# First SAGE pass of a graph network: stored turned blocks in place of transposes, seven masks in the first slots, one adjacency test moved to the gated part

## The chip, the cores and the metric

The kernel runs on one core of a Trainium2 chip. The metric is the device time of one execution in microseconds. The median of three runs of the kernel before is 2209.74 us (2208.95 to 2210.49).

## The reference

Input are 16 graphs of 1024 nodes with 128 features each, `x`, and their adjacency matrices `adj` (0 or 1, float32, not symmetric). Two layers follow each other. The first is a gated graph network: four rounds in which messages are summed over the adjacency and go through a GRU cell, then a residual sum and a layer norm. The second first thins the adjacency row by row ("neighbour skipping") and then runs three SAGE layers with batch norms over all graphs, a linear head, and again a residual sum and a layer norm.

```python
def _dilate_pattern(adj_bool, mask_b):
    def step(carry, n):
        row = carry[n]; num = sum(row)
        sf = where(num > 10, (num + 1) // 2, 1)
        rm = row & (cumsum(row) % sf == 0)          # only where num > 1
        carry[n] = row & ~rm
        carry[:, n] = carry[:, n] & ~rm             # later rows lose these too
    ...
def _sage(x, adj, Wr, Wx, b, mf):
    deg = clip(sum(adj, -1), 1.0)
    out = (adj @ x / deg) @ Wr + x @ Wx + b
    return out / max(norm(out), 1e-12) * mf
h = x
for i in range(4):
    h = gru_cell(adj.T @ (h @ weight[i]), h, ...)
x = layernorm(x + h * mask)
adj_d = adj * keep(adj)                             # the skipping
h1 = bn(relu(_sage(x, adj_d, ...))); h2 = ...; h3 = ...
out = layernorm(x + (concat(h1, h2, h3) @ Wl + bl) * mf)
```

An entry of the thinned matrix survives only if both its own row and the row of its column keep it. That is why both a block and its mirror image, turned, are needed.

## The kernel before

The work falls into five stages. Inside each the order of the instructions on every engine is the order in which the code emits them, so the tables and `if t in (...)` lines below are the schedule.

*Gated part* (0 to 1281 us). Two streams of graphs take turns; `Gated.layer` emits one layer of one stream. A layer is some 19 us, 64 layers in all. At ten places of a layer (`aside(n)`) one step of the skipping, `FixPoint.steps`, is emitted. The skipping works on blocks of 128 rows of four graphs at once (32 blocks of 20 steps, so a block lasts two layers): `keep` applies the removals that earlier rows of the graph have caused, from the tile `f_rt` (tile `left[i, g]`, 128 rows by k x 128 columns for block k); `count` scans; later `rows` writes the result `f_nr` to DRAM (`e_nr`, L867): +0.5 for an entry that its row keeps, -0.5 for one that it removes, 0 where there was no edge. `read_last` (L723) and `read_back` (L716) fill the next block's `f_rt` with DMA transposes of what earlier blocks wrote. There are four `f_rt` buffers. The kernel computes the skipping with a fixed point and with the assumption that `adj` holds only 0 and 1. `look` (L1982, VectorE, 128x1024) tests that assumption on a tile of 128 rows of `adj`; two of the eight tiles of a graph are tested in the gated part (`load_test`, `check`; tile `h_test`, one per layer of the second stream), six in the first SAGE pass (`load_a`, `check`; tile `p_a`).

*First SAGE pass* (`Sage.first`, 1281 to 1748 us). It runs over graphs, 16 slots for each: `slot(b, t)` emits slot t of graph `b` ("now") and at the same time prepares graph `n = b + 1` ("next"). The slots of b = -1 only prepare graph 0; this is the prologue. To prepare a graph is: load `e_nr` (`load_nr`, tile `p_nr`) and the rows (`load_s`, tile `p_s`); in `unit`, TensorE turns 128x128 blocks (four into one PSUM bank `p_u`, 16 units a graph, L1482); ScalarE writes the part above the diagonal into the thinned, transposed matrix `p_at` (L1487); in `unit_low` VectorE masks the rest (L1495: one input from `p_nr`, one from the PSUM bank); GpSimd packs each half row block to bytes (`pack`, L1503, tile `p_b`) for the later passes; the rows are normed, turned and split into a high and a low part (`p_xh`, `p_xl`). For "now", TensorE multiplies `p_at` with `p_xh` and `p_xl` (`agg`, L1564), then `out_first`, and then a chain goes through VectorE `scale_rows` (L1388, L1389), ScalarE `squares`, VectorE `rows` (L1402 to L1407), `split_r` on ScalarE and GpSimd (`p_rh`, `p_rl`), back to TensorE for the second aggregation (`agg` with `p_rh`, `p_rl`), and `turn_r`. `constants` and `first_weights` prepare weights; `load_given` loads them.

*Second and third pass and the head* (1748 to 2206 us) are not touched.

SyncE (SP) issues nearly all DMAs of the SAGE passes, in the order of the code; an issue that waits for a buffer holds up those behind it.

## Time and profile before

| what | value |
|---|---|
| median of three runs | 2209.74 us |
| the profiled execution's own time | 2207.94 us |
| its span, first to last instruction | 2206.2 us |
| granted TensorE clock, mean | 0.986 |
| busy: PE, DVE, ACT, POOL | 2099.8, 1836.0, 1327.2, 1233.9 us |
| gated part | 0 to 1281 us |
| first SAGE pass (prologue to 1296) | 1281 to 1748 us |
| second, third pass, head | 1748 to 2000, 2130, 2206 us |

PE is TensorE, PEld its weight loads, DVE VectorE, ACT ScalarE, POOL GpSimd, SP SyncE. A line such as `L1495 DVE ... p_at<-p_nr,p_u 128x512 fp32r<-128x512 bf16 x72 | 48.2, 673 | 3.5` is a group of 72 instructions of line 1495 that write `p_at` from `p_nr` and `p_u`; together they are busy 48.2 us, one takes 673 ns on average, and before them the engine was idle 3.5 us in all. Consecutive instructions of an engine may overlap by some 0.05 to 0.09 us.

### The profile page before, as it was taken

How to read it: one execution, taken by the hardware profiler on the slowest of the kernel's cores; microseconds unless marked ns; L12 is line 12 of the kernel's file. 1: busy time of each engine (PE TensorE's matmuls, PEld its weight loads, DVE VectorE, ACT ScalarE, POOL GpSimd, SP SyncE). 2: the span in 40 equal slices, each digit the busy share in tenths (PEclk: the TensorE clock that was granted, in tenths of full speed). 3: DMA queues.
4: the chain of work that ended last, by engine and by line, in shares of the span. 5: the costliest groups of instructions: out<-in, count | busy, mean ns of one | idle time of the engine just before them, and what ended most of it. 6: DMA issues, size and time to landing. Idle time of an engine off the chain costs nothing. (4 is left out here: it accounts for less than half of the span.)

```text
span 2206.2 us, 32924 instructions
## 1 busy us (share of the span) xinstructions
PE 2099.8 (95%) x10217; PEld 1441.5 (65%) x10217; DVE 1836.0 (83%) x4213; ACT 1327.2 (60%) x3238; POOL 1233.9 (56%) x1218
## 2 busy tenths in 40 slices
PE   6999999999999999999999979999999899999987
PEld 4666556666666665666655657777777678887865
DVE  4898998889998889989889978888888666766877
ACT  3657466565656666465575656666666355555756
POOL 4458558567476475585575457777777255540002
PEclk9999999999999999999999989999999999999989
DMA  8247446366364394472584178888887577764404
GB/s 254 76 107 244 90 115 223 85 179 184 84 202 129 80 256 110 91 241 78 126 237 101 52 263 309 304 306 306 305 305 259 210 249 248 248 225 171 139 30 143
DMA packets 233853, 406.13 MB, mean 184 GB/s; under 512 B 79042, under 2 KB 100196, under 8 KB 233668
## 3 DMA queue, kind: packets, MB, share of 16 engines
q1 hardware_dynamic: 187844, 284.37, 39.4%
q0 software_dynamic: 41472, 117.46, 19.8%
q10 hardware_dynamic: 4352, 2.11, 0.4%
q8 instruction: 83, 1.36, 0.2%
q14 instruction: 102, 0.84, 0.1%
HBM read 313.48 MB, written 109.25 MB: 192 GB/s over the span
## 5 line engine op out<-in xcount | busy, mean ns | idle before, releaser
L1104 PE MATMUL h_g<-h_h,h_wh 128*128 128x512 f32 x768 | 396.1, 597 | 3.3 <-DVE h_r L1116 3.3
L1104 PE MATMUL h_g<-h_ms,h_wi 128*128 128x512 f32 x768 | 392.2, 592 | 0.0
L1123 POOL TENSOR_TENSOR h_zh<-h_r,h_h 128x512 f32<-128x512 f32 x126 | 174.2, 1382 | 257.2 <-ACT h_r L1119 254.0
L737 DVE TENSOR_TENSOR_SCAN f_rank<-f_a,f_first,f_pd 128x1024 f16<-128x1024 bf16 x128 | 299.4, 2345 | 4.2
L1092 PE MATMUL h_g<-h_a,h_hi 128*128 128x512 f32 x1024 | 278.7, 413 | 1.0 <-DMA h_a<-in_adj_dram 0.9
L1503 POOL CAST p_b<-p_at 128x512 uint8<-128x512 f32 x256 | 219.8, 881 | 84.7 <-DVE p_at L1495 52.7
L1104 PEld LDWEIGHTS h_g<-h_ms,h_wi 128*128 128x128 f32 x768 | 145.5, 190 | 184.3 <-issue 168.9
L1092 PE MATMUL h_g<-h_a,h_lo 128*128 128x512 f32 x1024 | 261.8, 392 | 0.0
L1092 PEld LDWEIGHTS h_g<-h_a,h_hi 128*128 128x128 f32 x1024 | 190.1, 188 | 61.7 <-issue 22.2
L1396 ACT ACTIVATE s_junk<-s_o 128x128 bf16<-128x128 f32 x384 | 114.0, 298 | 175.2 <-DVE s_o L1389 164.6
L1092 PEld LDWEIGHTS h_g<-h_a,h_lo 128*128 128x128 f32 x1024 | 189.8, 188 | 38.6 <-DVE h_lo L1030 0.4
L1104 PEld LDWEIGHTS h_g<-h_h,h_wh 128*128 128x128 f32 x768 | 133.3, 190 | 100.3 <-issue 72.7
L1125 POOL TENSOR_TENSOR h_h<-h_h,h_zh 128x512 f32<-128x512 f32 x126 | 179.9, 1428 | 9.9
L1119 ACT ACTIVATE h_r<-h_r,h_bi 128x512 f32<-128x512 f32 x128 | 92.4, 722 | 149.2 <-DVE h_r L1118 149.2
L1124 POOL TENSOR_TENSOR h_zh<-h_z,h_zh 128x512 f32<-128x512 f32 x126 | 162.1, 1287 | 9.9
L1095 ACT COPY h_ms<-h_g 128x512 f32<-128x512 f32 x128 | 73.8, 577 | 150.8 <-PE h_g L1092 150.6
L910 ACT ACTIVATE f_u<-f_rank,f_q 128x128 f16<-128x128 f16 (+7 forms) x128 | 110.6, 867 | 70.2 <-DVE f_rank L850 70.2
L1771 PE MATMUL q_ob<-s_wxp,q_xt 128*128 128x256 f32 x512 | 125.7, 390 | 0.3
L1982 DVE SCALAR_TENSOR_TENSOR p_junk<-p_a 128x1024 bf16<-128x1024 f32 x96 | 125.7, 1309 | 0.0
L1495 DVE SCALAR_TENSOR_TENSOR p_at<-p_nr,p_u 128x128 fp32r<-128x128 bf16 (+1 forms) x192 | 102.5, 543 | 19.4 <-ACT p_at L1487 12.6
L887 ACT ACTIVATE f_pd<-f_rank,f_q 128x128 f32<-128x128 f16 x128 | 59.1, 462 | 96.5 <-DVE f_q L701 93.4
L1413 POOL TENSOR_TENSOR q_rl<-s_r,q_rh 128x512 fp32r<-128x512 f32 x32 | 41.2, 1288 | 128.8 <-ACT q_rh L1412 105.8
(256 smaller groups left out, 4770.7 us busy)
## 6 DMA issues: line engine op xcount, KB each, us to landing
h_a<-in_adj_dram POOLq DMA_DIRECT2D x128, 512.0 KB, 9.2
p_a<-in_adj_dram SPq DMA_DIRECT2D x96, 512.0 KB
f_a<-in_adj_dram POOLq DMA_DIRECT2D x128, 256.0 KB, 6.5
e_nr<-f_nr SPq DMA_DIRECT2D x128, 256.0 KB
p_nr<-e_nr SPq DMA_DIRECT2D x32, 1024.0 KB
h_test<-in_adj_dram SPq DMA_DIRECT2D x32, 512.0 KB
s_at<-p_b SPq DMA_DIRECT2D x32, 512.0 KB
s_ag<-s_ag SPq DMA_DIRECT2D x64, 256.0 KB
```

Of the source, the lines that this page charges most:

```text
L737: nc.vector.tensor_tensor_scan(out, a, other[:, 0, 0:1].to_broadcast([P, N]), start, op0=ALU.add, op1=ALU.bypass)
L910: nc.scalar.activation(u[:, :n1], rank[:, g, :n1], AF.Abs, bias=q[:, 1, g:g + 1], scale=q[:, 0, g:g + 1])
L1092: nc.tensor.matmul(pm[f], part[:, j, :], st.adj[j][:, half[f]], start=(j == 0 and n == 0), stop=(j == NB - 1 and n == 1))
L1104: nc.tensor.matmul(pg, lhs, rhs, start=(i == 0), stop=(i == len(mm) - 1))
L1123: aid.tensor_tensor(d, r, h, ALU.subtract)
L1124: aid.tensor_tensor(d, z, d, ALU.mult)
L1125: aid.tensor_tensor(h, h, d, ALU.add)
L1396: self.nc.scalar.activation(junk, o[:, i, :], AF.Square, accum_out=ss[:, i:i + 1])
L1495: self.nc.vector.scalar_tensor_tensor(g["at"][:, j, c0:c0 + low], v[:, j, c0:c0 + low], 0.0, pu[:, :low], op0=ALU.is_lt, op1=ALU.is_lt)
L1503: self.nc.gpsimd.tensor_copy(g["b", f][:, j, :], g["at"][:, j, f * HF:(f + 1) * HF].bitcast(F32))
L1771: nc.tensor.matmul(pb[:, i], g["xt"][:, f, blk], self.wxp, start=(i % 2 == 0), stop=False)
L1982: nc.vector.scalar_tensor_tensor(junk, a, 0.0, a, op0=ALU.is_gt, op1=ALU.not_equal, accum_out=bad[:, c:c + 1])
```

## The change

The skipping stores, for each block, the `f_rt` tile that it used in a new DRAM tensor `e_vt`: after step 10 of a block `send` issues four DMAs from SP. The tile's buffer is so held until the DMA has read it.

The first pass loads, for a graph, the lower blocks and the diagonal ones from `e_nr` in eight DMAs of 128 rows, and the 28 turned blocks from `e_vt` in one. TensorE then turns only the 36 blocks on and below the diagonal, in 12 units. VectorE masks the eight diagonal blocks from PSUM as before (`unit_own`) and the rest of each row block, 128 to 896 columns, in one instruction from the two loaded tiles (`unit_low`, seven of them, both inputs in SBUF). `p_at` is eight tiles in place of one.

The slots are laid out anew by four tables: units 0 to 3 stand in slots 0 and 2, the seven masks in slots 0 to 4 and (the last) 10. `out_first`, `scale_rows`, `rows`, `split_r` and the second aggregation each come one or two slots earlier. Five tests a graph stay in the pass; the sixth goes to the gated part, where each layer of the second stream now tests two tiles while the graphs 0, 1, 4, 5, 8, 9, 12, 13 run, and one as before in the others. `load_given` stands at the start of the pass, `constants` in slot 8 and `first_weights` in slot 9 of the prologue (it was in slot 3 of graph 0); the copy of `mask48` moves from `first_weights` to slot 4 of graph 0. The stores of `s_ag`, `s_at`, `s_rt`, `s_x` stand in other slots.

```diff
+def below(k):
+    return k * (k - 1) // 2
...
+    def send(self, i):
+        k, b0 = self.todo[i]
+        if k:
+            for g in range(self.G):
+                self.nc.sync.dma_start(self.turned[b0 + g, :, below(k) * P:below(k + 1) * P],
+                                       self.left[i, g][:, :k * P])
...
-            rt = self.left.pop((i, g))
+            rt = self.left[i, g]
...
             self.count(i, 1, a[1], rank, pt)
+            self.send(i)
...
     def load_test(self, n):
-        if n < B * 2:
-            self.test = self.wk.tile([P, N], F32, name="h_test", bufs=1)
-            self.nc.sync.dma_start(self.test, self.adj[n // 2, n % 2 * P:(n % 2 + 1) * P, :])
+        for i in range(1 + (n % NB < NB // 2)):
+            b, k = self.todo.pop(0)
+            t = self.wk.tile([P, N], F32, name="h_test")
+            self.nc.sync.dma_start(t, self.adj[b, k * P:(k + 1) * P, :])
+            self.tests.append((t, b, k))
...
-            if n == 1 and s == 1 and not checked:
-                self.check(b0 // 2 * L0 + l)
-                checked.append(l)
+            if s == 1 and self.tests and n not in checked and (n == 1 or n == 0 and len(self.tests) > 1):
+                self.check()
+                checked.append(n)
...
     def load_nr(self, b, f):
...
+            for k in range(4 * f, 4 * f + 4):
+                self.nc.sync.dma_start(g["v"][k], self.not_r[b, k * P:(k + 1) * P, :(k + 1) * P])
+                if k == 4:
+                    self.nc.sync.dma_start(g["low"], self.turn[b])
...
+        first, end = max(4 * f, j), 4 * f + 4
         pu = self.ps2.tile([P, HF], F32, name="p_u")
-        for i in range(4):
+        for i, k in enumerate(range(first, end)):
...
+    def unit_own(self, b, j):
+        g, own = self.g[b], slice(j * P, (j + 1) * P)
+        self.mask(g["at"][j][:, own], g["v"][j][:, own], g.pop(("pu", j)))
+
+    def unit_low(self, b, j):
+        g = self.g[b]
+        self.mask(g["at"][j][:, :j * P], g["v"][j][:, :j * P], g["vt"][j])
...
+    UNITS = {0: (0, 1), 2: (2, 3), 5: (8,), 6: (9,), 7: (10,), 8: (11,), 9: (12,), 10: (13,), 11: (14,), 12: (15,)}
+    LOWER = {0: (1, 2), 1: (3,), 2: (4,), 3: (5,), 4: (6,), 10: (7,)}
+    PACKS = {1: (0, 1), 3: (2, 3), 4: (4,), 5: (5,), 6: (6, 8), 7: (9,), 8: (10,), 9: (11,),
+             10: (12,), 11: (7, 13), 12: (14,), 13: (15,)}
+    TESTS = {1: 3, 5: 4, 7: 5, 11: 6, 13: 7}
...
-            if t in (5, 7):
-                self.out_first(b, t // 7)
+            if t in (4, 6):
+                self.out_first(b, t // 6)
...
-            if t in (9, 10, 12, 14):
-                part = g["rl"] if t in (10, 14) else g["rh"]
+            if t in (8, 9, 11, 12):
+                part = g["rl"] if t in (9, 12) else g["rh"]
...
+        if (b, t) == (-1, 8):
+            self.constants()
+        if (b, t) == (-1, 9):
+            self.first_weights()
         if (b, t) == (-1, 11):
-            self.load_given()
+            self.load_mask()
...
-        if (b, t) == (0, 3):
-            self.first_weights()
+        if (b, t) == (0, 4):
+            nc.vector.tensor_copy(self.mask48, self.m48)
```

## The prediction, made before the changed kernel ran

> **What bounds the kernel now.** I read the page's parts 1 and 2, then the windows by stage, the waits of the first SAGE pass, and one period of that pass as a timeline of VectorE and of GpSimd.

> Windows view; columns are stretch, length, busy us of PE, PEld, DVE, ACT, POOL, granted clock, DMA share, GB/s:

> ```profile
> 15.00:20.00 5.00, 1.12 (x4) 0.72 (x4) 0.42 (x2) 0.00 (x0) 0.53 (x1) 1.00 1.13 385
> ...
> 90.50:109.60 19.10, 19.10 (x75) 11.61 (x73) 15.32 (x36) 13.48 (x24) 8.40 (x8) 1.00 0.20 66
> 109.60:128.30 18.70, 18.70 (x70) 11.57 (x69) 17.86 (x38) 8.91 (x17) 9.53 (x11) 1.00 0.52 95
> ...
> 594.20:613.30 19.10, 19.10 (x75) 11.61 (x73) 17.23 (x37) 14.62 (x26) 10.07 (x9) 1.00 0.28 91
> ...
> 1552.40:1580.10 27.70, 26.25 (x193) 20.96 (x192) 24.33 (x62) 17.84 (x51) 20.16 (x21) 1.00 0.88 299
> ```

> The gated part (0 to 1281 us) is TensorE's: its layers last 18.7 to 20.5 us and PE fills them, with DVE busy 15 to 19 us of each. The start is DMA's: between 5 and 25 us the DMA engines are full and PE waits for weights. The last row is one graph of the first pass (1296 to 1748 us; from one graph's scale_rows to the next's the intervals average 27.79 us). There PE (26.25), DVE (24.33) and DMA (0.88) are all nearly full, so none alone sets the period. PE's own rest, in the waits view of that pass over 16 graphs (us in total, times, longest), is the chain of scale_rows, squares, rows and split; the third line is graph 0's alone:

> ```profile
> PE p_ag L1564 <- POOL p_rl L1413: 12.2, 15, 0.9
> PE p_ag L1564 <- ACT p_rh L1412: 10.1, 16, 1.8
> ...
> DVE s_mask L1310 <- DMA p_a<-in_adj_dram: 2.8, 1, 2.8
> ```

> **The change part by part.**

> *Transposes.* A unit of four blocks takes PE 0.20 to 0.23 us from its start to the next operation's (1555.33 to 1555.53), 0.053 a block. 28 fewer: 1.5 us, so PE needs 24.8 us a graph. This is a gain only if nothing else holds the period.

> *DVE work.* One test of six leaves: 1.31 + 0.08 us. Groups by form, over 12.25 graphs:

> ```profile
> L1982 DVE SCALAR_TENSOR_TENSOR p_junk<-p_a 128x1024 bf16<-128x1024 f32 x75 | 98.3, 1310 | 0.0
> ...
> L1495 DVE SCALAR_TENSOR_TENSOR p_at<-p_nr,p_u 128x512 fp32r<-128x512 bf16 x72 | 48.2, 673 | 3.5 <-PE p_u L1482 3.5
> L1495 DVE SCALAR_TENSOR_TENSOR p_at<-p_nr,p_u 128x384 fp32r<-128x384 bf16 x25 | 13.6, 545 | 6.2 <-ACT p_at L1487 6.2
> L1495 DVE SCALAR_TENSOR_TENSOR p_at<-p_nr,p_u 128x256 fp32r<-128x256 bf16 x25 | 10.5, 421 | 1.5
> L1495 DVE SCALAR_TENSOR_TENSOR p_at<-p_nr,p_u 128x128 fp32r<-128x128 bf16 x25 | 6.8, 272 | 0.0
> ```

> The twelve masks of a graph now take 6.5 us. The same 36 blocks come as eight own blocks (8 x 0.27 = 2.2) and seven masks of 128 to 896 columns. On the line of the rows above (0.27, then 0.133 per 128 columns) the seven are 4.7 us; by the gated part's f_a masks, which like them read both inputs from SBUF, 5.2 (0.35 at 128 columns, 1.10 at 896). So masks rise by 0.4 to 0.9 and DVE's work goes from 24.33 to between 23.3 and 23.8; I take 23.6.

> *The new conflict.* The old masks read one input from SBUF and one from PSUM; the seven new ones read two from SBUF. Timeline of DVE (start, length, line, operation):

> ```profile
> 609.64 1.08 DVE L729 SCALAR_TENSOR_TENSOR f_a<-f_rt,f_a 128x896 bf16<-128x896 bf16 x1
> ...
> 1552.72 1.55 DVE L1982 SCALAR_TENSOR_TENSOR p_junk<-p_a 128x1024 bf16<-128x1024 f32 x1
> ...
> 1560.13 1.21 DVE L1982 SCALAR_TENSOR_TENSOR p_junk<-p_a 128x1024 bf16<-128x1024 f32 x1
> ```

> and of GpSimd at the same times:

> ```profile
> 609.97 1.89 POOL L1123 TENSOR_TENSOR h_zh<-h_r,h_h 128x512 f32<-128x512 f32 x1 [1.58 <-ACT h_r L1119]
> 611.94 1.27 POOL L1124 TENSOR_TENSOR h_zh<-h_z,h_zh 128x512 f32<-128x512 f32 x1
> ...
> 1559.95 1.87 POOL L1503 CAST p_b<-p_at 128x512 uint8<-128x512 f32 x1 [2.67 <-DVE p_at L1495]
> 1562.01 0.62 POOL L1503 CAST p_b<-p_at 128x512 uint8<-128x512 f32 x1 [0.19 <-DVE s_rdeg L1559]
> ```

> A pack that meets a test lasts 1.87 us where the next, beside masks that read PSUM, lasts 0.62; a test that meets a pack lasts 1.55 in place of 1.21; the f_a mask holds up h_zh by 0.6 us. So a DVE instruction with two SBUF inputs and a GpSimd one take turns. Each new mask can cost DVE nothing or one whole pack (0.6 us): 0 to 4.2 us a graph. I take half, 2.1, because packs of the columns just masked become ready exactly when the next mask starts. DVE's work is then about 25.7 us.

> *DVE's idle time.* Of 3.4 us a period, the timeline shows 0.90 for a mask waiting for ACT's half of p_at, which goes; 0.37 for p_rs, 0.21 for s_ss, 0.76 and 0.22 for s_rt and small gaps stay. With about 1.7 kept the period is 25.7 + 1.7 = 27.4 us. GpSimd is the cross-check: 16 packs of 0.6 and four splits of 1.28 are 14.7 us, and DVE's two-SBUF instructions (five tests 6.0, seven masks 4.7, two rows 1.4, small ones 0.8) 12.9; taking turns that is 27.6, less about 1 to 2 us because consecutive starts overlap by 0.05 to 0.09. So 26 is a floor and 27.4 plausible; PE, at 24.8, becomes a waiter.

> [...]

> *DMA.* Turned blocks and the lower parts of e_nr are 28 + 36 blocks, the 2 MB loaded before; one test less is 0.5 MB of about 8.3. At 27.4 us that is about 284 GB/s against 299. The rows of 256 and 512 bytes are few. SP issues some six more DMAs a graph at 0.3 to 0.45 us and is mostly idle. load_a waits on SP for a test's buffer, and behind it stand the stores of s_rt, s_ag and s_at; each buffer's test lies one slot or more earlier, so I charge nothing; if that cover went, pack 0 of the next graph would wait for its p_b buffer, some 2 us, with GpSimd 7.5 us idle in a period.

> *First weights.* Now they, with mask48's copy, sit inside graph 0: from its first p_xh matmul (1296.42) to its scale_rows (1314.66) it takes 18.2 us, a later graph 11.4. That excess of 6.8 goes, the 2.8 us wait of s_mask with it. But constants (2.7 us of DVE) and first_weights (2.9, with PE between) move into the prologue, ahead of the last masks; its DVE has 4.5 us of waits to hide them in, and the p_u banks hang on those masks. I add 2.5 us (0 to 4). Net -4.3.

> *Gated part.* 16 tests of 1.2 to 1.5 us come into layers of the second stream of graphs 0-1, 4-5, 8-9, 12-13. Such layers have 3.8 us of DVE idle (90.5 to 109.6: 19.10 less 15.32) beside 1.9 in the heavy ones (594.2), and stay PE-bound; the first such layer of each pair of graphs has 2.3 to 3.3. I charge 0.8 us in all; 0 to 8; 21 if the cover were gone. 112 sends (SP, 0.4 us each) stand behind the transposes into f_rt that they wait for, and read_back waits for their landing; but read_back waits for DVE's f_a anyway, tens of us later for most. Nothing, up to 3 us. At the start a second test tile, 0.5 MB, is loaded while DMA is full: 0.52 MB at 250 to 385 GB/s is 1.4 to 2.1 us before PE's first layer: +1.6.

> *Sum.* 15 x (27.4 - 27.79) = -5.9; -4.3; +0.8; +1.6: -7.8 us. The profiled execution took 2207.94 (span 2206.20); the median is 1.8 above. From the median: 2202 us.

> **The rivals.**

> *The port decides (slower).* If the masks wait for three quarters of a pack each (3.2 us; all of it, 4.2, is the bound), the period is 23.6 + 3.2 + 1.7 = 28.5 (29.5): 15 x 0.7 = +10.6, with -4.3 and +2.4: +8.7, 2218 us. Slower by over 0.2% it is from a period of 28.2 on. For it: GpSimd is busy 20.16 of 27.70, and its order puts p_xl, for which PE waits, behind packs. Against: a mask that directly follows another need not wait, since the pack of 1559.95 waited through two DVE instructions.

> *No conflict.* The masks cost what the p_at rows say: DVE 23.6 + 1.7 = 25.3, and PE, 24.8 with its present 1.4 us of waits, sets 26.2. 15 x -1.6 = -23.9, less 1.9: 2184 us. Against: the f_a row.

> *The period stays.* The loop of scale_rows, squares, rows and splits sets it as before: -4.3 + 2.4, 2208 us, no change that shows.

> *The gated part pays.* The tests push DVE past its idle time in half of the 16 layers, 10 us: 2212.

> **How the numbers follow.** Forecast 0.36, no conflict 0.17, period stays 0.13, port 0.27, gated 0.07. 0.2% is 4.4 us, about what a measurement can tell from no change. Faster: 0.17 and 0.33 of the forecast's 0.36, 0.50. Same: the rest of it and most of "stays", 0.15. Slower: 0.35. The range from 2181 to 2221 leaves out the tails of the first and the port case.

> **What would show it.** L1482 at 576 transposes, PE at about 25 us a period; the seven masks at 5 us or more in a graph, packs of p_b at over 1 us mean; scale_rows of graph 0 near 1311; 48 tests in the gated part, ending within 3 us of 1281. Wrong it would be if the period is under 26.5 or over 28.2, or if PE shows new waits in the gated part.

## The result: 2.65% slower, and where the 56 us are

The changed kernel takes 2265.65 us (median of four runs, 2263.84 to 2266.44) against 2209.34 for the kernel before: ratio 1.0265, 95% interval 1.0249 to 1.0281. The forecast was 2202, the range 2181 to 2221. The profiled execution of after took 2263.84 us (span 2261.6), 55.9 us more than that of before.

By stage, from the two traces. The gated stretch ends with the last layer's last sums (the expectations below call that the last layer's start); graph times run from one first p_xh matmul to the next:

| stage | before | after | difference | forecast |
|---|---|---|---|---|
| start to first gated aggregation | 33.7 | 35.1 | +1.4 | +1.6 |
| gated part from there | 1227.3 | 1239.2 | +11.9 | +0.8 |
| to its last turn | 18.8 | 19.1 | +0.3 | 0 |
| prologue of the first pass | 16.6 | 34.2 | +17.6 | +2.5 |
| graph 0 | 34.5 | 28.3 | -6.2 | -6.8 |
| graphs 1 to 14 | 389.4 | 413.4 | +24.0 | -5.5 |
| graph 15 and all behind it | 485.8 | 492.3 | +6.5 | -0.4 |

Of the last row, 5.8 us lie in graph 15 itself (to the first matmul of the next layer's weights: 29.7 before, 35.5 after).

Windows of after, columns as in the prediction (length, busy us of PE, PEld, DVE, ACT, POOL, granted clock, DMA share, GB/s):

```profile
15.00:20.00 5.00, 1.46 (x7) 0.77 (x5) 0.56 (x1) 0.00 (x0) 1.01 (x2) 1.00 1.13 380
91.90:111.00 19.10, 19.10 (x75) 11.61 (x73) 17.45 (x38) 13.44 (x23) 9.31 (x8) 1.00 0.23 76
600.10:619.20 19.10, 19.10 (x75) 11.59 (x73) 17.20 (x37) 14.59 (x26) 10.03 (x9) 1.00 0.31 108
1355.89:1384.40 28.51, 25.02 (x168) 19.50 (x166) 24.52 (x63) 17.26 (x52) 23.20 (x21) 1.00 0.81 277
1384.40:1414.45 30.05, 26.56 (x168) 20.58 (x166) 24.49 (x63) 17.27 (x52) 22.36 (x21) 0.94 0.77 263
```

The light layer of graph 1 (second row) still lasts 19.10, with the second test inside it: DVE 17.45 instead of 15.32. So the cover named in the prediction held there. The last two rows are two neighbouring graphs of the first pass. PE has its forecast 25 us, DVE 24.5. But the graph lasts 28.5 us where the clock is 1.00 and 30.05 where it is 0.94; nine of the graphs 1 to 14 are of the second kind. Before, PE's waits were 1.4 us a graph (1.41 on the mean of graphs 1 to 14); now they are 3.5, and over all sixteen the longest are:

```profile
PE p_ag L1600 <- POOL p_xl L1433: 31.2, 15, 2.8
PE p_u L1509 <- DVE p_at L1519: 12.5, 16, 0.9
PE p_ag L1600 <- ACT p_rh L1432: 11.8, 16, 1.4
```

The first line was not there before: PE stands 2.03 us in each of the graphs 1 to 14, waiting for p_xl. Groups by form of the pass (graphs 1 to 14):

```profile
L1536 POOL CAST p_b<-p_at 128x512 uint8<-128x512 f32 x224 | 243.0, 1117 | 34.2 <-issue 12.8 <-DVE p_sh L1558 7.2 <-DMA s_at<-p_b 5.2
L1519 DVE SCALAR_TENSOR_TENSOR p_at<-p_nr,p_u 128x128 fp32r<-128x128 bf16 x112 | 28.5, 274 | 15.0 <-ACT p_at L1513 15.0
L1519 DVE SCALAR_TENSOR_TENSOR p_at<-p_nr 128x640 fp32r<-128x640 bf16 x14 | 17.2, 1225 | 0.0
L1519 DVE SCALAR_TENSOR_TENSOR p_at<-p_nr 128x896 fp32r<-128x896 bf16 x14 | 15.0, 1072 | 0.0
```

Packs take 1117 ns on the mean, before 901; the seven masks sum to 5.76 us a graph, and the one of 640 columns takes longer than that of 896, so what stands beside it counts.

### The profile page after: what moved, and what is told of

It reads as the page before. It is cut to its first block, busy times and chain, and to the rows that moved or that the text cites. A ratio compares the mean times of both kernels' runs of the same rounds, so it can differ in the third digit from the quotient of the medians.

```text
span 2261.6 us, 32358 instructions
## 1 busy us (share of the span) xinstructions
PE 2094.8 (93%) x9769; PEld 1424.3 (63%) x9769; DVE 1879.0 (83%) x4261; ACT 1314.6 (58%) x3238; POOL 1287.3 (57%) x1218
## 3 DMA queue, kind: packets, MB, share of 16 engines
q8 instruction: 80, 1.31, 0.2%
## 5 line engine op out<-in xcount | busy, mean ns | idle before, releaser
L1536 POOL CAST p_b<-p_at 128x512 uint8<-128x512 f32 x256 | 273.2, 1099 | 56.1 <-DVE p_at L1519 20.8
L1142 POOL TENSOR_TENSOR h_zh<-h_z,h_zh 128x512 f32<-128x512 f32 x126 | 176.8, 1403 | 9.9
L1055 PEld LDWEIGHTS h_g<-ident,h_h 128*128 128x128 f32 x512 | 62.7, 142 | 74.8 <-issue 68.5
L2027 DVE SCALAR_TENSOR_TENSOR p_junk<-p_a 128x1024 bf16<-128x1024 f32 x80 | 108.7, 1359 | 0.0
```

The lines of the kernel that those rows point to most:

```text
L1142: aid.tensor_tensor(d, z, d, ALU.mult)
L1536: self.nc.gpsimd.tensor_copy(g["b", f][:, j, :], g["at"][j][:, f * HF:(f + 1) * HF].bitcast(F32))
L2027: nc.vector.scalar_tensor_tensor(junk, a, 0.0, a, op0=ALU.is_gt, op1=ALU.not_equal, accum_out=bad[:, c:c + 1])
```

## Experiments

Theories after the result: the loss is four separate things (a pool's edge in the prologue, the second tests in the gated part, a longer loop in the first pass, a lowered clock on top). Rivals: the sends pay the gated part, the weights' loads the prologue, and the conflict of masks and packs the pass. Ratios are to the kernel before, run on the same chip. In the code below `...` marks lines left out, and comments name the run that a line belongs to.

**own_pool**: a pool of their own for two tiles.

```diff
         self.wk = pool("h_wk", bufs=2)
+        self.tp = pool("h_tp", bufs=2)      # h_test and h_junk from here
...
```

> The changed kernel with h_test and h_junk in a pool of their own behind the gated part's work pool; same addresses, same instructions. Theory A (the second h_test moves the end of the gated part's work pool 4 KB up, from 160320 to 164416 bytes a partition, over the start of the first p_nr at 162912, and the first load of p_nr then waits for the last use of any tile of that pool, the store of h_x): load_nr starts within 5 us of the last e_nr store, as before (there 1267.59 after a store at 1263.41 to 1267.1), the time from the gated part's last turn to the first p_xh aggregation falls from 34.9 to 17-20 us, the whole to 2247-2252. Rival B (the weights' loads and first_weights, now inside the prologue, hold it): that stretch stays above 28 us and the whole above 2258.

Ratio 1.0185 (1.0163 to 1.0208), 2248.1 us. SP's timeline (start, us, issue) of before, after and own_pool, in this order; with after stands GpSimd's issue of the last store of h_x:

```profile
1263.41 3.71 SPq L867 DMA_DIRECT2D e_nr<-f_nr  x4
1267.59 0.96 SPq L1466 DMA_DIRECT2D p_nr<-e_nr  x2
```

```profile
1276.59 3.71 SPq L881 DMA_DIRECT2D e_nr<-f_nr  x4
1296.07 0.54 POOL L1090 DMA_DIRECT2D e_sum<-h_x  x1 [8.46 <-DVE h_x L1088]
1299.16 0.82 SPq L1491 DMA_DIRECT2D p_nr<-e_nr  x2
```

```profile
1278.52 3.72 SPq L881 DMA_DIRECT2D e_nr<-f_nr  x4
1282.74 2.26 SPq L1492 DMA_DIRECT2D p_nr<-e_nr  x5
```

In after the load stands 18.9 us behind the last store of e_nr: SP waits until the store of h_x, issued 3.1 us earlier, has landed (its waits on the stores of h_x: 18.5 us). In own_pool it stands half a microsecond behind. The prologue is 22.1 us instead of 34.2. What PE waited for in after:

```profile
1300.96 0.27 PE L1509 MATMUL p_u<-ident_b,p_nr 128*128 128x128 bf16 x1 [7.16 <-DMA p_nr<-e_nr]
1313.11 0.58 PE L1509 MATMUL p_u<-ident_b,p_nr 128*128 128x128 bf16 x4 [8.68 <-DVE p_at L1519]
```

Theory A is shown for 12.1 of the 17.6 us: the second h_test, 4 KB, pushed the work pool's end over p_nr's first bytes (by the addresses that the expectation gives), and the load into that ground waited for the last user of the whole pool. In mended, below, with one h_test and no pool of its own, the prologue is 22.0 us too. (The 22.1 miss the 17 to 20 foretold by 2; see before_early.)

**one_test** and **no_sends**: the two additions to the gated part, taken away one at a time.

```diff
-        for i in range(1 + (n % NB < NB // 2)):
-            b, k = self.todo.pop(0)
+        for b, k in [(n // 2, n % 2)]:          # one_test
...
-            self.send(i)                        # no_sends
```

> The changed kernel without the sixteen second tests of the gated part (k = 2 of each graph is left untested; two h_test buffers stay, so addresses are the same). Theory A (DVE's time for the second test is what the gated part pays): first aggregation to last layer's start falls from 1238.9 us to 1227-1230 (before: 1227.1), the whole to 2253-2257. Rival B (the 112 sends pay it, by the places they take on SP ahead of the read-backs and by their DMA): that stretch stays within 2.5 us of 1238.9, the whole above 2261.

> The changed kernel without the sends of turned blocks (the first pass reads as many bytes from e_nr in their place, in pieces of 1 KB, so its masks hold other values). Theory A (second tests on DVE pay): the gated stretch of 1238.9 us falls by at most 3, the whole to no less than 2261. Rival B (sends pay): it falls by 8 to 12, to 1227-1231, the whole to 2253-2258.

In no_sends the first pass reads as many bytes from e_nr as it read from e_vt, so its masks hold other values. one_test: ratio 1.0202 (1.0182 to 1.0222), gated stretch 1228.7. no_sends: 1.0244 (1.0223 to 1.0265), stretch 1241.6. The second tests pay, all of it as far as the runs can tell; the sends cost nothing that shows. (Over all runs the stretch is 1238.8 to 1244.3 with the second tests and 1227.0 to 1229.4 without, with sends or not.) DVE at the end of graphs 8 and 9, before and then after:

```profile
792.05 1.30 DVE L1982 SCALAR_TENSOR_TENSOR h_junk<-h_test 128x1024 bf16<-128x1024 f32 x1
803.36 1.14 DVE L729 SCALAR_TENSOR_TENSOR f_a<-f_rt,f_a 128x512 bf16<-128x512 bf16 x1 [1.91 <-DMA f_rt<-f_nr]
```

```profile
797.22 2.00 DVE L2027 SCALAR_TENSOR_TENSOR h_junk<-h_test 128x1024 bf16<-128x1024 f32 x1
801.08 1.74 DVE L2027 SCALAR_TENSOR_TENSOR h_junk<-h_test 128x1024 bf16<-128x1024 f32 x1
812.97 1.75 DVE L742 SCALAR_TENSOR_TENSOR f_a<-f_rt,f_a 128x512 bf16<-128x512 bf16 x1 [2.50 <-DMA f_rt<-f_nr]
```

Two tests last 3.7 us where one lasted 1.30. The layer that holds them keeps its 19.8 us, but DVE leaves it late: f_w, f_nr and the transposed read behind them come later, the f_a mask that waits for that read starts 18.7 us into the layer instead of 16.8, and the scans behind it run into the next layer, the first one of graph 10, which is already full. That layer takes 22.94 us, before 20.07. (In one_test it still takes 21.72, the mask starting 17.6 us in; so in this layer alone the test accounts for 1.2 of the 2.9 us, and it is the whole stretch that shows its price.) PE's waits for these scans (f_x) grow in the gated part from 1.1 us in all to 6.8.

**small_packs**: packs of 64 columns in the changed kernel, into two tiles that are set to zero once.

```diff
-        self.nc.gpsimd.tensor_copy(g["b", f][:, j, :], g["at"][j][:, f * HF:(f + 1) * HF].bitcast(F32))
+        self.nc.gpsimd.tensor_copy(g["b", f][:, j, :64], g["at"][j][:, f * HF:f * HF + 64].bitcast(F32))
```

> The changed kernel with each of the 256 packs of p_b cut to 64 of its 512 columns (the rest of s_at is zero, so the later passes add up other values). Theory A (GpSimd and DVE take turns on SBUF, which stretches packs to 1.1 us and puts p_xl, queued behind them, late for PE): the period of the first pass falls from 28.5 to 25.5-27 us in graphs at full granted clock, PE's wait for p_xl (28.4 us in 14 graphs) nearly goes, the whole is 25 to 45 us shorter. Rival B (the period comes from the chain of scale_rows, squares, rows and split, or from the granted clock): periods stay within 0.5 of 28.5 and 30.05, the whole within 8 us.

Ratio 1.0216 (1.0193 to 1.0239); the graphs last 28.4 and 29.95. That is rival B, though the whole is 10 us shorter where B had at most 8. PE's wait for p_xl went, and another took its place: that for p_rl's row of node degrees, which ACT copies and PE turns into columns (waits of PE, graphs 1 to 14):

```profile
PE s_tr L1596 <- ACT p_rl L1586: 33.8, 14, 2.6
```

**turned_only**, **turned_small_packs**, **before_small_packs**: the turned blocks in the slots of the kernel before; the same with small packs; and the kernel before with small packs, as a control.

```diff
+        first, end = max(4 * f, j), 4 * f + 4            # the slots of before, 36 blocks turned
...
+        if 4 * f <= j < 4 * f + 4:
+            mask(slice(j * P, (j + 1) * P), g.pop("pu")[:, :P])
+        lo, hi = 4 * f * P, min(j, 4 * f + 4) * P
+        if lo < hi:
+            mask(slice(lo, hi), vt[:, lo:hi])
```

> The kernel before with the turned blocks alone: sends, the load of lower parts and turned blocks, 36 transposes and masks from SBUF, in the slots, the order and the places of the kernel before (six tests in the pass, one h_test, first_weights in graph 0; twelve masks become eighteen, since a block's own part and its lower part are taken apart). Theory A (the rearranged slots cost the pass, the blocks themselves gain): periods 26.5-27.3 instead of 27.73, the gated part within 3 us of before, the whole 2190-2203. Rival B (masks with two SBUF inputs cost more than transposes save): periods 28-29, the whole 2212-2230.

> turned_only (period 28.93, packs 1028 ns, masks of 512 columns 903 ns) with each pack cut to 64 of its 512 columns, so that GpSimd hardly reads SBUF (the rest of s_at is zero). Theory A (masks and packs take turns on SBUF, and that is what the masks cost in these slots): the period falls to 27.0-27.8, masks of 512 columns to 0.70-0.75 us. Rival B (it is the number of masks, eighteen for twelve, and their place before scale_rows): the period stays above 28.4.

> The kernel before with each pack cut to 64 of its 512 columns (the rest of s_at zero): the control for turned_small_packs, which fell from 28.93 to 27.6 us a graph. Theory A (the conflict belongs to the masks that read SBUF twice): the period stays 27.4-27.75, the whole within 5 us of before. Rival B (packs cost the pass as much before): the period falls by 1 us or more.

| mean of graphs 1 to 14, us | full packs | small packs |
|---|---|---|
| transposes of 64 blocks (before) | 27.81 | 27.58 |
| turned blocks, eighteen masks, ten of them from SBUF | 29.05 | 27.54 |

Ratios 1.0099 (1.0081 to 1.0117) for turned_only, 1.0009 (0.9998 to 1.0021) for turned_small_packs, 1.0003 (0.9992 to 1.0014) for the control. Small packs gain 0.23 us a graph before and 1.51 with the new masks, so 1.3 us a graph is the conflict that the prediction named. The masks themselves show it, in turned_only and then in turned_small_packs:

```profile
L1517 DVE SCALAR_TENSOR_TENSOR p_at<-p_nr 128x512 fp32r<-128x512 bf16 x52 | 45.9, 903 | 0.0
```

```profile
L1520 DVE SCALAR_TENSOR_TENSOR p_at<-p_nr 128x512 fp32r<-128x512 bf16 x52 | 35.1, 695 | 0.0
```

The right column of the table says more: with the conflict out, the turned blocks gain nothing (27.54 against 27.58). Either PE's 28 transposes were not on the path, or the six more masks took their gain back (DVE works 24.9 us a graph in turned_small_packs, 23.8 in before_small_packs); no run parts the two.

**filler**: six matmuls more in each graph, just ahead of PE's wait.

```diff
+                if t == 1 and b >= 1:
+                    idle = bank()
+                    for j in range(6):
+                        nc.tensor.matmul(idle, self.xh[:, j, :], g["at"][j][:, :HF], start=(j == 0), stop=(j == 5))
```

> The changed kernel with six more matmuls of PE (p_xh times p_at, some 1.6 us, into a bank that nobody reads) at the start of the p_xl aggregation of graphs 1 to 15, where PE otherwise stands still for 2.03 us. Theory A (the 2.03 us of standing still is what lowers the granted clock: ten graphs of 30.05 us have 3.41 us at 0.5 just behind it, five of 28.5 have none): no low clock in the pass, all periods 28.5 +/- 0.3, the pass 424-431 instead of 441.7 us, the whole 10 to 18 us shorter though work was added. Rival B (the clock falls for another reason, such as the load or DMA): about as many periods of 30 stay, or more, and the whole is no shorter.

Ratio 1.0189 (1.0167 to 1.0212): some 15 us faster than the changed kernel, with more work. PE of after behind the wait, in a graph of 30.05 and in one of 28.5:

```profile
1478.20 1.20 PE L1600 MATMUL p_ag<-p_at,p_xl 128*128 128x512 f32 x4 [2.04 <-POOL p_xl L1433]
1479.39 3.66 PE L1600 MATMUL p_ag<-p_at,p_xh 128*128 128x512 f32 x8
```

```profile
1419.57 1.20 PE L1600 MATMUL p_ag<-p_at,p_xl 128*128 128x512 f32 x4 [2.04 <-POOL p_xl L1433]
1420.76 2.09 PE L1600 MATMUL p_ag<-p_at,p_xh 128*128 128x512 f32 x8
```

The same eight matmuls take 3.66 us or 2.09. In the first kind the trace's clock records show 3.41 us at a granted clock of 0.50 behind the wait (1479.47 to 1482.88); half of 3.41 us lost in 30.05 leaves the row's 0.94. In filler none of the graphs 1 to 14 has it; the first two:

```profile
1359.87:1388.38 28.51, 26.34 (x174) 20.65 (x172) 24.55 (x63) 17.28 (x52) 23.36 (x21) 1.00 0.80 277
1388.38:1416.88 28.50, 26.35 (x174) 20.64 (x172) 24.52 (x63) 17.29 (x52) 23.29 (x21) 1.00 0.81 277
```

So of the 24.0 us of graphs 1 to 14, 14.3 (the mean of 29.53 less filler's 28.51, times 14) are the lowered clock and 9.8 (28.51 less 27.81) the longer loop. That PE's 1.3 us of extra work left the graph at 28.5 shows that PE's load does not set it.

**What holds 28.5.** Eight runs took loads away or moved single steps. Two of them have small packs as well (both_cut, light), and two have own_pool's pool (chain_cut, packs_late), so that their ratios hold its gain too:

```diff
-        if now and t in self.TESTS: ...                   # no_sage_tests, light (and its load_a)
-    TESTS = {1: 3, 5: 4, 7: 5, 11: 6, 13: 7}
+    TESTS = {1: (3,), 5: (4, 5), 7: (6,), 11: (7,)}       # tests_moved
+            if t > 13 and n + 1 < B:
+                self.norm_stats(n + 1, t - 14)            # norm_early, chain_cut, both_cut, packs_late
+            if nxt and t in (10, 12):
+                self.split_x(n, t // 12)                  # ahead of turn_r: chain_cut, packs_late
-             10: (12,), 11: (7, 13), 12: (14,), 13: (15,)}
+             10: (12,), 11: (13,), 13: (7, 14), 14: (15,)}   # packs_late
+        if now and b and t == 3:
+            nc.vector.bn_stats(self.stats[0][:, 2 * b - 1, :], self.rt_last)   # stats_late
```

> The changed kernel without the five tests of the first pass (rows 3 to 7 of blocks of each graph stay untested and are not loaded there). Theory A (DVE's work between graphs, tests, masks and norm_stats, holds ACT at p_rs for 4 us and with it the eviction, the degree row and p_xl: the period is DVE's and ACT's order, not PE and not GpSimd): periods fall from 28.5 to 25.5-26.5 and the low clock goes, the whole 45-70 us shorter. Rival B (the chain of PE, eviction, scale_rows, squares, rows, split sets it, whatever DVE does beside it): periods stay above 28.

> The changed kernel with the test of slot 13 moved to slot 5, behind the one there, where DVE waits 2.2 us for s_ss; nothing else. Theory A (DVE's order between graphs sets the period): the period falls by the test's 1.2-1.5 us to 27-27.4, the wait for p_xl below 1.2 us, so that the low clock goes too: the pass about 405-412 us instead of 441.7, the whole 28-38 us shorter. Rival B (not DVE's order): the period stays within 0.4 of 28.5 and 30.05.

> The changed kernel with norm_stats of the next graph issued in slots 14 and 15 of the graph before, ahead of the masks of slots 0 and 1 (there ACT waits 4.0 us a graph at p_rs for DVE's p_mv, with the eviction and the degree row queued behind it). Theory A (two chains of nearly the same length close the loop between graphs: s_tr, s_rt, p_xh on ACT, packs and p_xl on GpSimd; and masks, norm_stats, p_rs, eviction, degree row on ACT; cutting one leaves the other): ACT's wait at p_rs falls below 1.5 us a graph, yet the period stays within 0.6 of 28.5 and PE's wait for p_xl at 1.5 us or more. Rival B (the second chain alone sets the period): the period falls to 26-27.5, the whole 25 us or more shorter.

> norm_early, and split_x of slots 10 and 12 issued ahead of turn_r's copy on ACT (which waits 3.5 us for PE there) instead of behind it, and h_test and h_junk in a pool of their own as in own_pool. Theory A (two chains): with both cut the period falls to 25.8-27.3, no wait of PE over 1.3 us and no low clock in the pass (15 periods about 390-410 us instead of 441.7), the whole 2203-2222. Rival B (the masks' SBUF reads and DVE's 24.5 us hold the pass): periods 27.8 or more, the whole above 2232.

> norm_early and small_packs together (norm_stats ahead of the masks; packs of 64 columns, the rest of s_at zero). Theory A (two chains of nearly the same length close the loop; each alone left 28.3 to 28.4 us): the period falls to 25.8-27.4, no wait of PE over 1.4 us, no low clock in the pass; the pass 385-412 us instead of 441.7. Rival B (one chain that holds neither: PE, eviction, scale_rows, squares, rows, split, PE): period within 0.4 of 28.3.

> chain_cut with packs 7 and 14 in slot 13 and pack 15 in slot 14, so that p_xl of slot 12 stands ahead of three packs on GpSimd. Theory A (p_xl behind packs is the chain left in chain_cut, where PE waits 1.9 us for it): PE's wait for p_xl falls below 1 us, the period to 26.5-27.6 and the low clock goes: the pass 398-415 us instead of 435.1, the whole 2205-2225. Rival B: the wait moves to the degree columns or p_rh with 1.5 us or more, the period stays above 28.

> The changed kernel with the second bn_stats of s_rt (slot 12, where DVE waits 1.03 us for ACT's copy of PE's turn) issued in slot 3 of the next graph instead; the load of every engine is the same. Theory A (order: DVE's queue between slots 12 and 2 closes the loop): the period falls by 0.8 to 1.7 us from 28.5, PE's wait for p_xl by as much, and with it the low clock: the pass 400-425 us instead of 441.7. Rival B (load, or another loop): the period stays within 0.4 of 28.5 and 30.05.

> no_sage_tests and small_packs together: five tests a graph left out, packs of 64 columns (the rest of s_at zero), which leaves DVE about 17.5 us and GpSimd about 11 us of work a graph. Theory A (order): the period stays at 27.0-27.6, as in no_sage_tests, with engines idle a third of the time and PE still waiting 1.3 us or more in one place. Rival B (load): the period falls to 26 or below, PE's 24.8 us and its short waits.

| run | ratio (95%) | graph at full clock | PE's longest wait, for what | graphs 1 to 14 with low clock |
|---|---|---|---|---|
| no_sage_tests | 1.0129 (1.0111 to 1.0147) | 27.55 | 1.58, degree columns | 2 |
| tests_moved | 1.0307 (1.0289 to 1.0326) | 30.1 | 1.7, degree columns | 12 |
| norm_early | 1.021 (1.0192 to 1.0228) | 28.3 | 1.8, p_xl | 7 |
| chain_cut | 1.017 (1.0152 to 1.0188) | 28.3 | 1.9, p_xl | 8 |
| both_cut | 1.0256 (1.0239 to 1.0273) | 28.8 | 2.6, p_u behind masks | 11 |
| packs_late | 1.0137 (1.012 to 1.0154) | 28.3 | 0.76 and 0.82, 2 us apart | 6 |
| stats_late | 1.0266 (1.0249 to 1.0283) | 28.7 | 1.9, p_xl | 10 |
| light | 1.0109 (1.0091 to 1.0126) | 27.5 | 1.5, degree columns | 2 |

My first answer (DVE's load between graphs) fell with tests_moved, which was 1.6 us a graph worse in place of 1.3 better; the second (two chains) with both_cut and packs_late; the third (one wait in DVE's queue) with stats_late. In no_sage_tests five tests less took 1.0 us off a graph, which lies between its two theories. light decides the question in general: a graph of it has

```profile
1440.38:1467.85 27.47, 24.75 (x169) 19.61 (x166) 16.81 (x53) 17.28 (x52) 10.16 (x20) 1.00 0.52 192
```

DVE 16.8 and GpSimd 10.2 of 27.5, and still PE (first fence) waits at the degree columns for what ACT (second) does late, which in turn waits for DVE (third):

```profile
1439.59 0.60 PE L1438 MATMUL s_tr<-ident,s_r 128*128 128x128 f32 x4
1447.95 0.25 PE L1596 MATMUL s_tr<-s_one,p_rl 1*128 1x1 f16 x4 [1.49 <-ACT p_rl L1586]
```

```profile
1440.22 0.59 ACT L1639 COPY s_rt<-s_tr 128x512 f32<-128x512 f32 x1 [3.55 <-PE s_tr L1438]
1446.42 0.30 ACT L1558 ACTIVATE p_rs<-p_mv,s_eps 128x8 f32<-128x8 f32 x1 [3.45 <-DVE p_mv L1555]
1447.28 0.62 ACT L1586 CAST p_rl<-s_ag 1x512 f16<-1x512 f32 x1
```

```profile
1442.72 0.56 DVE L1522 SCALAR_TENSOR_TENSOR p_at<-p_nr,p_u 128x128 fp32r<-128x128 bf16 x2 [1.19 <-ACT p_at L1516]
```

This is a ring: PE's last turn (turn_r), ACT's copy of it, p_xh and evictions (copies of sums out of PSUM), DVE's masks and norm_stats (mean and variance of the next graph's rows), ACT's p_rs (their root), eviction and degree row, and back to PE at 1447.95, 8.4 us after the turn began at 1439.59; PE then goes on in order, with 1.2 us of shorter waits, for 19.1 us to the next turn at 1467.05. With DVE's tests in the same ring (the full kernel against no_sage_tests) it is 28.5. The new order's ring is thus about as long with most of the load gone as the old order's with all of it. In the changed kernel itself the trace leads back from PE's wait for p_xl another way: without a pause through GpSimd's packs (the two just behind p_rl take 3.93 us), from there to ACT's p_rh and DVE's rows and scale_rows, and to PE's aggregation that ended 20.7 us before (1457.53). So more than one ring is nearly as long, which fits that the runs that took one wait of PE away met another. That the order, and not the load of DVE or GpSimd, keeps light at 27.5 is shown; which of the moved slots made the rings longer is not: no single move found it.

**before_early** and **mended**: the one part whose stage gained, and the change without its costs in the gated part and the prologue.

```diff
+            self.load_given()                      # before_early: behind load_s(0), first_weights at (-1, 9)
...
-    TESTS = {1: 3, 5: 4, 7: 5, 11: 6, 13: 7}
+    TESTS = {1: 2, 5: 3, 7: 4, 9: 5, 11: 6, 13: 7}   # mended: packs_late's order, one h_test
```

> The kernel before with one part of the change alone: the weights' loads right behind load_s(0), first_weights in the prologue (slot 9), the mask's load in slot 11 and its copy in graph 0. Theory A (the part gains by itself, since SP is free there in the kernel before): graph 0's period 34.5 becomes 28 +/- 0.5, the prologue grows by 1 to 3 us, the whole 3 to 6 us shorter (2201-2205). Rival B (what graph 0 gains the prologue gives back, as it waits for the weights' loads): no difference over 2 us.

> The changed kernel with packs_late's order, and the sixth test back in the first pass (slots 1, 5, 7, 9, 11, 13) with one h_test as in the kernel before, so that the gated part has its 32 tests and its work pool ends where it did. Theory A: gated part as before +-2, prologue 20-23 us, the period 27-28 (1.3 us more of DVE than packs_late), no low clock in the pass: the whole 2200-2212, no more than 0.3% from before. Rival B (DVE's six tests and the masks' SBUF reads bind): period 28.5 or more, the whole above 2220.

before_early: ratio 1.0 (0.999 to 1.0011). Graph 0 falls from 34.5 to 29.1, the prologue grows from 16.6 to 20.6; what is left does not show. mended: 1.0111 (1.0095 to 1.0128); gated stretch 1229.4 and prologue 22.0 as foretold, but 28.9 us a graph, as rival B had it. No version beat the kernel before.

## Why the prediction was wrong

*Startup, sends, transposes.* Sends nothing, 576 transposes and PE at 25.0, now a waiter: right. At the start +1.4 for 1.6 is partly luck: the first aggregation begins at 33.7 to 35.2 us in the seven kernels that load one tile there and at 34.7 to 36.6 in the thirteen that load two, 0.9 us between the means.

*Steady period, 27.4.* The step that failed, twice. The sum "DVE's work 25.7 plus 1.7 kept idle" took DVE's load for the bound and its idle time for a constant. DVE's work came out at 24.5 and its idle time at 4.0, so the total of 28.5 is the one of the port rival, but not by its cause: small_packs left it. The period is that of rings through the queues of several engines, and the prediction never followed one round for the new slots. "The period stays" named part of that ring, but took it as unchanged.

*The new conflict, 2.1 us a graph.* That the new masks and the packs slow each other was right (in the old slots a mask of 512 columns takes 903 ns beside full packs, 695 beside small ones); the size was 1.3, measured in the old slots; in the new ones the rings hid it (small_packs). It was charged to DVE alone: the seven masks take 5.76 us where 4.7 to 5.2 were the price without it, and with the eight own blocks 7.9, 1.5 over before. GpSimd paid more: sixteen packs at 1117 ns in place of 901 are 3.5 us a graph.

*The clock.* Missing. The profile of before showed 1.00 in the graphs 1 to 14, and the prediction asked what waits cost but not what a wait of 2 us does behind itself: 14.3 us.

*First weights.* -6.8 was -6.2; +2.5 was 4.0 (before_early, 20.6 less 16.6), and own_pool's prologue, with the rest of the change, is 5.5 longer.

*Prologue.* The second h_test was charged 1.6 us of loading at the start and nothing more; what it does to the tiles behind it in memory was not asked: 12.1 us. The load of p_nr was taken to start where it did.

*Gated part, 0.8 (0 to 8).* Mis-sized, 11.9. A test was priced at 1.2 to 1.5 us, though the 32 in the gated part before had a mean of 1.54; the sixteen raise DVE's test time there from 49.3 to 85.1 us, 2.2 each. Before, the five tests with no GpSimd instruction beside them took 1.22 us each, the other 27 a mean of 1.60 and up to 2.16; that more of this stretching makes up the 2.2 is likely, and no run shows it alone. And the idle time was read in the layer alone, while the lateness crossed into the full layers of the next graphs.

*Graph 15.* It was counted as one more period; it lost 5.8 us. PE's waits in it grew from 6.5 to 10.4 us, and two half-clock stretches lie in it where before had one. Why the waits grew stays open in part: in packs_late, where the last packs stand behind p_xl, it takes 30.8, in chain_cut, which differs from it by that alone, 34.6.

## What to carry to other kernels

Follow the new order once round the ring before pricing a load: where no engine is full, taking work off one can move a wait and gain little (small_packs: 28.4 us a graph for 28.5). A buffer added to one pool can push it over the tiles of another (here 4 KB cost 12.1 us); compare addresses and see who waits for whose release. And price a wait of PE not only by its length but by the slow matmuls behind it (here eight took 3.66 us for 2.09): filling it with idle work can pay (filler: some 15 us).

## What the runs showed of the hardware

```profile
1476.06:1479.47 3.41, 1.37 (x9) 0.90 (x8) 3.41 (x19) 0.00 (x0) 2.97 (x4) 1.00 1.13 390
1418.03:1421.45 3.42, 1.88 (x10) 1.44 (x11) 3.05 (x19) 0.42 (x2) 2.37 (x3) 1.00 1.05 342
```

The others agree: ahead of each of the nine stretches PE stood idle for 1.99 to 2.05 of the 3.41 us, and in the five other graphs the larger part of the wait was 1.02 to 1.54 us. That 1.54 us is no bound: in graph 15 PE stood idle for 1.38 us of such a stretch (1786.67 to 1790.08), and the next 3.41 us have 0.50 too.

Across the runs, the longest wait and the number of the graphs 1 to 14 with low clock go together only roughly: none at up to 1.4 us (turned_only), two at 1.5 and at 1.6, seven at 1.8, eight to ten at 1.9 to 2.03 (six runs), nine at 2.4 (small_packs), eleven at 2.6. Two waits of 0.8 us within 3 us go with six (packs_late), one of 1.7 with twelve (tests_moved); why twelve there is not shown.
